# An attention-and-experts kernel on one core: TensorE in program order, output matmuls two tiles behind their energies

## The chip, the core and the metric

The kernel runs on one core of one Trainium2 chip. The core has a matrix engine (TensorE, PE in the profile, with its weight loads as PEld), three elementwise engines (VectorE or DVE, ScalarE or ACT, GpSimd or POOL), and a sync engine (SP), whose queue issues most of the transfers here. The engines run side by side and meet at semaphores. Matmuls write to PSUM, from which VectorE and ScalarE read. The metric is the device time of one execution in microseconds; of several runs the median counts.

## The reference, cut to what is computed

There are four images of 32 channels and 128 x 128 pixels. Layer 0 folds each 2 x 2 block of pixels into channels (128 channels, 64 x 64 = 4096 positions) and lets every position attend to all positions of its image. So an image has 4096 rows of length 128, and the energy is the 4096 x 4096 matrix of their cosines. Layer 1 works on the same data as 4096 tokens of 128 numbers per image.

```python
def _L0_conv_ref(x, gamma):                      # per image
    xs = x.reshape(B, C, h, R, w, R).transpose(0, 1, 3, 5, 2, 4).reshape(B, C * R * R, h, w)
    q = xs.reshape(B, C * R * R, hw)
    energy = jnp.einsum('bci,bcj->bij', q, q)
    d = jnp.sqrt(jnp.diagonal(energy, axis1=1, axis2=2))
    energy = energy / (d[:, :, None] * d[:, None, :])
    attn = jax.nn.softmax(energy, axis=-1)
    out = jnp.einsum('bcj,bij->bci', q, attn).reshape(B, C * R * R, h, w)
    out = gamma * out + xs
    ...
# layer 1
t = t + _L1_attn_ref(_ln_t(t), Wk, Wq, Wv)       # linear attention: a 128x128 matrix per image
t = t + _L1_ffn_ref(_ln_t(t), router_w, router_b, expert_w, expert_b)   # top 2 of 8 experts
```

The energy is symmetric, and so is its exponential. The kernel computes only one half of it, in tiles of 128 x 512, and gets the other half by transposing tiles.

## The kernel before: the parts that are touched

All is f32. The kernel is written with a scheduler: the program emits instructions in an order, and the scheduler decides in which order each engine gets them, by its own estimate of when each is ready. On the chip the order of every engine is then fixed, and semaphores make it wait.

An image's 4096 rows are 32 blocks of 128, or `NCH` = 8 chunks of 512. For chunk `i` ("a row") the kernel goes over the diagonal chunk and over the chunks `jc < i`. For each of four blocks `j` of such a chunk ("a tile") it makes an energy `pe`, its exponential `pr` on ScalarE, and the output matmul into `po`, which sums up over the whole row. The output matmul is held in `pend` and emitted after the next tile's energy.

```python
    ps_e = ctx.enter_context(tc.tile_pool(name="ps_e", bufs=2, space=PSUM))   # pe
    ps_o = ctx.enter_context(tc.tile_pool(name="ps_o", bufs=1, space=PSUM))   # po
    ps_g = ctx.enter_context(tc.tile_pool(name="ps_g", bufs=1, space=PSUM))   # pg
    ps_t = ctx.enter_context(tc.tile_pool(name="ps_t", bufs=2, space=PSUM))   # all transposes, and others
    ps_y = ctx.enter_context(tc.tile_pool(name="ps_y", bufs=2, space=PSUM))   # py, gram
    # ... cut ...
        for i in range(NCH):
            po = ps_o.tile([P, CH], F32, tag="po", name=f"po_{b}_{i}")
            # ... cut: order of chunks, pend, given, values, below ...
            for jc in order:
                # ... cut ...
                for j in range(NJ):
                    t = NJ * jc + j
                    c0 = 0 if jc < i else P * j
                    pe = ps_e.tile([P, CH], F32, tag="pe", name=f"pe_{b}_{i}_{t}")
                    nc.tensor.matmul(pe[:, c0:], qn[jc][:, ts(j, P)], qn[i][:, c0:], start=True, stop=True)
                    pr = ppool.tile([P, CH], F32, tag="pr", name=f"pr_{b}_{i}_{t}")
                    nc.scalar.activation(pr[:, c0:], pe[:, c0:], AF.Exp, accum_out=sums[:, t, i : i + 1])
                    flush()
                    if j == 1:
                        pend.extend(given)
                        given.clear()
                    pend.append(partial(values, pr[:, c0:], t, c0, CH))
                    if jc < i:
                        nc.vector.transpose(Fb[:, :, :, j, :], pr)
                    own.append(pr)
                    if jc == i and j in (1, 2):
                        pend.append(partial(below, own, (2, 1) if j == 1 else (3,)))
                    clock[0] += 2 * (CH - c0) // P
                    if late and late[0][0] <= clock[0]:
                        clock[0] += NJ
                        if next(late[0][1], "done") == "done":
                            late.pop(0)
                    yield
                if jc < i:
                    # ... cut: 16 transfers G <- F on SyncE ...
                    late.append((clock[0] + LAG, transposed_share(b, st, i, jc, G)))
            pend.extend(given)
            flush()
            o = opool.tile([P, CH], F32, tag="o", name=f"o_{b}_{i}")
            nc.vector.tensor_copy(o, po)
            st["o"].append(o)
```

In the diagonal chunk only the upper half of the tiles is computed. `below` makes the lower half: it transposes parts of `pr` on TensorE into `ptd`, ScalarE copies them to `gd`, and these go into output matmuls too (`given`).

For the chunks left of the diagonal, the transposed tiles are needed for another row's output. VectorE transposes `pr` in 32 x 32 squares into `F`, sixteen transfers put the squares in their places in `G`, and later (`LAG` in the kernel's own count of TensorE work) four matmuls `pg` are made of it, one after each tile; ScalarE sums up each part of `G` into `junk`, and VectorE adds `pg` to the other row's `o`.

Between tiles (at the `yield`) other streams take steps: the preparation of the next image (transposes `ptq`, `ptn`, and squares, norms and scaling `ss`, `rn`, `qs` on VectorE and GpSimd), and layer 1 of the image before. A stream gets a stretch of the image, in per cent of its work, and a count of steps.

```python
        else:
            streams.append((layer1(b - 1, states[b - 1], False), 7, 97, 161))
```

Layer 1 divides the output by the row sums (`pbd`, `df`), adds it to the tokens `T`, takes each token's mean and variance (`bs_a`, `dm_a`, the power on GpSimd for `rsa`, then `nba`), normalises on ScalarE, eight tokens' columns at once, and forms a Gram matrix `pgram`:

```python
        for kc in range(6):
            if kc < 4:
                yield from divide(kc)
            if 1 <= kc < 5:
                yield from row_stats(f"a{b}", kc - 1, rsa, nba)
                yield
                for k in range(8 * kc - 8, 8 * kc):
                    normalise(xn[:, k, :], k, rsa, nba)
                yield
            if 2 <= kc:
                gram_rows(kc - 2)
                yield
```

Then follow the attention product `pat`, a second normalisation into `xg`, its transposes `ptf`, routing, and the experts: for each of 32 token blocks two matmuls `py` of 128 x 512, with the bias from `pbe` and the gates transposed by `ptg`. The last image's layer 1 runs alone, after all attention is done.

Of the kernel before, what the change touches and what calls it, by code (L numbers as in the profile page):

```python
# [10 lines left out]
F32 = mybir.dt.float32  # L11
# [8 lines left out]
def kernel(  # L20
# [35 lines left out]
    nc = tc.nc  # L56
    P = 128
# [3 lines left out]
    CH = 512  # L61
    NCH = N // CH
    NJ = CH // P
# [11 lines left out]
    opool = ctx.enter_context(tc.tile_pool(name="opool", bufs=NCH + 2))  # L75
# [6 lines left out]
    ps_o = ctx.enter_context(tc.tile_pool(name="ps_o", bufs=1, space=PSUM))  # L82
# [4 lines left out]
    def psum_t(name):  # L87
        return ps_t.tile([P, CH], F32, tag="pt", name=name)
# [71 lines left out]
    def prep(b, kc, st):  # L160
# [35 lines left out]
        for s, qs in enumerate(scaled):  # L196
# [5 lines left out]
            st.setdefault("qn", {})[2 * kc + s] = qn  # L202
            yield

    late = []
    clock = [0]
    LAG = 56
# [19 lines left out]
    def attend(b, st):  # L227

        qT, qn = st.setdefault("qT", {}), st.setdefault("qn", {})
        st["sums"] = sums = stat.tile([P, NB, NCH + 1], F32, tag="sums", name=f"sums_{b}")  # L230
        nc.gpsimd.memset(sums[:, :, NCH:], 0.0)
        st["o"] = []

        for i in range(NCH):
            po = ps_o.tile([P, CH], F32, tag="po", name=f"po_{b}_{i}")
            ending = b == B - 1 and i == NCH - 1
            order = list(range(i)) + [i] if ending else [i] + list(range(i))
            pend, given = [], []
            count = [0]
            total = NJ * (i + 1) + NJ - 1  # L240

            def values(w, blk, lo, hi, i=i, po=po, count=count, total=total):
                count[0] += 1
                nc.tensor.matmul(  # L244
                    po[:, lo:hi], qT[blk // NJ][:, blk % NJ, :], w, start=(count[0] == 1), stop=(count[0] == total)
                )

            def below(tiles, blks, i=i, given=given):

                pt = psum_t(f"ptd_{b}_{i}_{blks[0]}")  # L250
                gd = ppool.tile([P, CH], F32, tag="pr", name=f"gd_{b}_{i}_{blks[0]}")
                at = 0
                for ib in blks:
                    for j in range(ib):
                        nc.tensor.transpose(pt[:, at + P * j : at + P * j + P], tiles[j][:, ts(ib, P)], ident)  # L255
                    w = gd[:, at : at + P * ib]
                    nc.scalar.activation(
                        w, pt[:, at : at + P * ib], AF.Copy, accum_out=sums[:, NJ * i + ib, NCH:]
                    )
                    given.append(partial(values, w, NJ * i + ib, 0, P * ib))  # L260
                    at += P * ib

            def flush(pend=pend):
                while pend:
                    pend.pop(0)()

            for jc in order:
                if jc < i:
                    F = fpool.tile([P, 4, NJ, NJ, S], F32, tag="F", name=f"F_{b}_{i}_{jc}")
                    Fb = F.rearrange("p q ib j c -> p ib q j c")  # L270
                own = []
# [4 lines that stand above are left out]
                    nc.tensor.matmul(pe[:, c0:], qn[jc][:, ts(j, P)], qn[i][:, c0:], start=True, stop=True)  # L276
                    pr = ppool.tile([P, CH], F32, tag="pr", name=f"pr_{b}_{i}_{t}")
                    nc.scalar.activation(pr[:, c0:], pe[:, c0:], AF.Exp, accum_out=sums[:, t, i : i + 1])  # L278
                    flush()
                    if j == 1:  # L280
                        pend.extend(given)
                        given.clear()
                    pend.append(partial(values, pr[:, c0:], t, c0, CH))
                    if jc < i:
                        nc.vector.transpose(Fb[:, :, :, j, :], pr)  # L285
                    own.append(pr)
                    if jc == i and j in (1, 2):
                        pend.append(partial(below, own, (2, 1) if j == 1 else (3,)))
                    clock[0] += 2 * (CH - c0) // P
                    if late and late[0][0] <= clock[0]:  # L290
                        clock[0] += NJ
# [4 lines that stand above are left out]
                    G = gpool.tile([P, 4, NJ, P], F32, tag="G", name=f"G_{b}_{i}_{jc}")  # L296
                    for a in range(4):
                        for q in range(4):
                            nc.sync.dma_start(  # L299
                                G[ts(q, S), a].rearrange("p ib f -> p (ib f)"),  # L300
                                F[ts(a, S), q].rearrange("p ib j c -> p (ib j c)"),
                            )
                    late.append((clock[0] + LAG, transposed_share(b, st, i, jc, G)))
                    st["due"] = st.get("due", 0) + 1
            pend.extend(given)
            flush()
            o = opool.tile([P, CH], F32, tag="o", name=f"o_{b}_{i}")
            nc.vector.tensor_copy(o, po)
            st["o"].append(o)

    def finish_late():
        while late:
            for _ in late.pop(0)[1]:
                pass


    def layer1(b, st, alone):
# [51 lines left out]
        def normalise(dst, k, rs, nb):  # L369
            nc.scalar.activation(dst, T[:, k, :], AF.Identity, scale=rs[:, k, :], bias=nb[:, k, :])  # L370
# [40 lines left out]
        def gram_rows(u):  # L411
            for k in range(8 * u, 8 * u + 8):
                nc.tensor.matmul(pgram[:, :D], xn[:, k, :], xn[:, k, :], start=(k == 0), stop=(k == KT - 1))  # L413
# [6 lines that stand above are left out]
                yield  # L420
                for k in range(8 * kc - 8, 8 * kc):
                    normalise(xn[:, k, :], k, rsa, nba)
                yield
            if 2 <= kc:
                gram_rows(kc - 2)
                yield
                if alone:
                    transpose_rows(2 * kc - 4)
                    transpose_rows(2 * kc - 3)
# [139 lines left out]
        for g in range(KT // 4):  # L569
# [5 lines left out]
            for jj in range(2):  # L575
                tmp = work.tile([P, 2, 4, D], F32, tag="wide", name=f"tmp_{b}_{g}_{jj}")
                for jk in range(2):
                    j = 2 * jj + jk
                    k = 4 * g + j
# [26 lines left out]
    states = [{} for _ in range(B)]  # L606
# [6 lines left out]
        pass  # L613
    carried = []

    for b in range(B):

        streams = list(carried)
        carried = []
        if b == 0:  # L620
            for kc, begin, end in ((1, 0, 5), (2, 6, 20), (3, 25, 45)):
                streams.append((prep(0, kc, states[0]), begin, end, 10))
            streams.append((setup_weights(), 50, 60, 4))
        else:
            streams.append((layer1(b - 1, states[b - 1], False), 7, 97, 161))
        if b + 1 < B:
            nxt = states[b + 1]
            streams.append((prep(b + 1, 0, nxt), 66, 84, 10))
            streams.append((prep(b + 1, 1, nxt), 85, 99, 10))
            carried.append((prep(b + 1, 2, nxt), 2, 20, 10))  # L630
            carried.append((prep(b + 1, 3, nxt), 30, 50, 10))
        done = [0] * len(streams)
        start = clock[0]
        for _ in attend(b, states[b]):
            t = 100 * (clock[0] - start) / UNITS
            for n, (steps, begin, end, count) in enumerate(streams):
                while t >= begin and done[n] * (end - begin) < (t - begin) * count:
                    next(steps, None)
                    done[n] += 1
        for steps, *_ in streams:  # L640
            for _ in steps:
                pass
    finish_late()
    last = states[B - 1]
    for _ in layer1(B - 1, last, True):
        pass
# [38 lines left out]
```

## Time and profile before

| | before |
|---|---|
| device time, median of 3 | 1890.58 us (1890.11 to 1890.69) |
| span of the profiled execution | 1886.6 us |
| mean granted TensorE clock | 0.983 |
| matmul records on TensorE | 5474 |
| ScalarE exp, 128x512 | 560 ns mean, and 199 ns to read its sum |
| VectorE transposes `F` | 704 ns mean, 448 of them |
| transfers `G` from `F` | 1792, 64 KB each |

The profile is one execution. In a timeline each line has the start, the time in us, the engine, the line of the kernel, the operation, what it writes and reads, its shape and how many records are merged; in brackets stand the idle time of that engine before it and what ended it. An f32 matmul of 128 x 512 appears as two records, a transpose as one. In the slices of the page each digit is a fortieth of the span, in tenths. Since TensorE is nearly always at work, the small gaps between its records matter more here than the shares.

### The profile page before, as it was taken

To read this page: it belongs to the slowest core of one execution; us is meant where nothing else is said; L and a number is where in the kernel's file an instruction comes from. 1 tells how busy PE (TensorE), PEld (TensorE's weight loads), DVE (VectorE), ACT (ScalarE), POOL (GpSimd) and SP (SyncE) were. 2 spreads that over 40 slices of the span, in tenths; PEclk is the share of its full clock that TensorE was granted. 3 is DMA by queue.
4 is the path that set the end of the run, shared out by engine and by line. 5 is a ranking of instruction groups with operands and counts; after the bars stand their busy time and mean duration, and the time that the engine had idled before them with its cause. 6 is when DMAs were issued, how large, how long until landed. Compare 5 with 4: busy or idle time off the path is not lost.

```text
span 1886.6 us, 21105 instructions
## 1 busy us (share of the span) xinstructions
PE 1799.0 (95%) x5474; PEld 915.4 (49%) x5474; DVE 909.5 (48%) x2201; ACT 974.6 (52%) x3117; POOL 293.7 (16%) x279
## 2 busy tenths in 40 slices
PE   6999999998999999999999999999899999999678
PEld 4444544454555444455555444445465544444533
DVE  3343224345364454636355455453536445554576
ACT  3454444446457454555556655454554755554455
POOL 0000000002010122212000022220300012221336
PEclk9999999999999999999999999999999999999789
DMA  5333343332233232342233323234233223335001
GB/s 119 80 84 87 78 104 91 89 89 64 61 95 83 65 89 65 86 105 64 64 85 81 92 62 90 68 88 99 53 79 81 72 63 92 81 74 119 1 11 34
DMA packets 142247, 145.68 MB, mean 77 GB/s; under 512 B 32528, under 2 KB 84784, under 8 KB 142128
## 3 DMA queue, kind: packets, MB, share of 16 engines
q1 hardware_dynamic: 138496, 142.73, 31.5%
q10 hardware_dynamic: 3632, 1.60, 0.4%
q8 instruction: 45, 0.74, 0.2%
q14 instruction: 74, 0.61, 0.1%
HBM read 18.38 MB, written 8.39 MB: 14 GB/s over the span
## 4 chain that ended last, share of the span: by engine, by line
PE 81%; DVE 7%; SPq 4%; POOL 3%; ACT 2%; DMA 1%; issue 1%; ACTq 0%; POOLq 0%; DVEq 0%
PE po L244 23%; PE pe L276 20%; PE pg L213 18%; PE py L588 5%; PE py L581 5%; SPq L299 4%; PE pbe L571 1%; PE pat L468 1%; PE pgram L413 1%; DVE F L285 1%; PE ptd L255 1%; POOL rsa L111 1%; DVE df L387 1%; POOL T L395 1%; PE ptn L199 1%
## 5 line engine op out<-in xcount | busy, mean ns | idle before, releaser
L278 ACT ACTIVATE pr<-pe 128x512 f32<-128x512 f32 (+1 forms) x576 | 322.7, 560 | 519.6 <-PE pe L276 513.9
L244 PE MATMUL po<-pr,qT 128*128 128x512 f32 (+3 forms) x1152 | 551.1, 561 | 16.4 <-ACT pr L278 11.6
L285 DVE STREAM_TRANSPOSE F<-pr 128x512 f32<-128x512 f32 x448 | 311.4, 704 | 354.0 <-ACT pr L278 336.5
L276 PE MATMUL pe<-qn,qn 128*128 128x512 f32 x896 | 459.7, 595 | 0.0
L213 PE MATMUL pg<-G,qT 128*128 128x512 f32 x896 | 440.8, 594 | 1.7 <-DVE o L223 1.6
L244 PEld LDWEIGHTS po<-pr,qT 128*128 128x128 f32 x1152 | 213.3, 191 | 249.0 <-issue 182.9
L218 ACT ACTIVATE junk<-G 128x512 bf16<-128x512 f32 x448 | 277.1, 626 | 3.6 <-DMA G<-F 2.8
L213 PEld LDWEIGHTS pg<-G,qT 128*128 128x128 f32 x896 | 167.4, 191 | 196.0 <-issue 186.8
L590 ACT ACTIVATE tmp<-py,gate 128x128 f32<-128x128 f32 x512 | 146.3, 368 | 172.1 <-PE py L588 171.1
L583 DVE SCALAR_TENSOR_TENSOR acc<-py,gate,acc 128x128 f32<-128x128 f32 x512 | 177.7, 349 | 118.3 <-PE py L581 104.6
L276 PEld LDWEIGHTS pe<-qn,qn 128*128 128x128 f32 x896 | 160.9, 191 | 145.3 <-issue 144.4
L223 DVE TENSOR_TENSOR o<-o,pg 128x512 f32<-128x512 f32 x112 | 76.6, 684 | 184.4 <-PE pg L213 183.7
L594 POOL TENSOR_TENSOR tmp<-tmp 128x512 f32<-128x512 f32 x64 | 81.2, 1269 | 534.6 <-ACT tmp L590 534.6
L581 PE MATMUL py<-ew_sb,xn 128*128 128x512 f32 x256 | 132.7, 601 | 1.9 <-ACT tmp L590 1.2
L588 PE MATMUL py<-ew_sb,xn 128*128 128x512 f32 x256 | 131.9, 597 | 2.2 <-DVE acc L583 1.4
L278 ACT ACTIVATION_READ_ACCUMULATOR pr<-pe 128x1 f32 x576 | 114.5, 199 | 0.0
L111 POOL TENSOR_TENSOR rn<-ss,neg_half 128x8 f32<-128x8 f32 x16 | 26.2, 1639 | 500.4 <-DVE ss L185 500.4
L276 PE MATMUL pe<-qn 128*128 128x512 f32 (+3 forms) x256 | 90.3, 444 | 0.0
L218 ACT ACTIVATION_READ_ACCUMULATOR junk<-G 128x1 f32 x448 | 88.5, 198 | 0.0
L370 ACT ACTIVATE xn<-T,nba,rsa 128x128 f32<-128x128 f32 x128 | 51.9, 481 | 55.1 <-DVE nba L367 55.1
L111 POOL TENSOR_TENSOR rsf<-dm_f,neg_half 128x8 f32<-128x8 f32 x16 | 26.3, 1642 | 342.5 <-DVE dm_f L365 342.5
L588 PEld LDWEIGHTS py<-ew_sb,xn 128*128 128x128 f32 x256 | 48.5, 191 | 61.9 <-issue 53.0
(121 smaller groups left out, 1416.5 us busy)
## 6 DMA issues: line engine op xcount, KB each, us to landing
G<-F SPq DMA_DIRECT2D x1792, 64.0 KB, 2.0
xx<-in_x_dram SPq DMA_DIRECT2D x64, 128.0 KB, 2.8
T<-in_x_dram SPq DMA_DIRECT2D x16, 512.0 KB, 7.1
out_dram<-acc SPq DMA_DIRECT2D x128, 64.0 KB, 1.8
ew_sb<-in_L_ffn_expert_w_dram ACTq DMA_DIRECT2D x1, 512.0 KB, 5.4
raw_w<-in_L_attn_Wv_dram ACTq DMA_DIRECT2D x1, 512.0 KB
raw_w<-in_L_attn_Wk_dram ACTq DMA_DIRECT2D x1, 256.0 KB
raw_w<-in_L_attn_Wq_dram ACTq DMA_DIRECT2D x1, 256.0 KB
```

The lines of the kernel that those rows point to most:

```text
L213: nc.tensor.matmul(pg.rearrange("p (a f) -> p a f", a=4), st["qT"][i][:, ib, :], G[:, :, ib], start=(ib == 0), stop=(ib == NJ - 1),)
L218: nc.scalar.activation(junk, G[:, :, ib], AF.Copy, accum_out=st["sums"][:, NJ * i + ib, jc : jc + 1])
L223: nc.vector.tensor_tensor(o, o, pg.rearrange("p (a j c) -> p a j c", a=4, c=S), ALU.add)
L244: nc.tensor.matmul(po[:, lo:hi], qT[blk // NJ][:, blk % NJ, :], w, start=(count[0] == 1), stop=(count[0] == total))
L276: nc.tensor.matmul(pe[:, c0:], qn[jc][:, ts(j, P)], qn[i][:, c0:], start=True, stop=True)
L278: nc.scalar.activation(pr[:, c0:], pe[:, c0:], AF.Exp, accum_out=sums[:, t, i : i + 1])
L285: nc.vector.transpose(Fb[:, :, :, j, :], pr)
L581: nc.tensor.matmul(py, xn[:, k, :], ew_sb[:, 0:4, :], start=True, stop=True)
L583: nc.vector.scalar_tensor_tensor(acc[:, j, :], py[:, ts(e, D)], gate[:, k, e : e + 1], acc[:, j, :], ALU.mult, ALU.add)
L588: nc.tensor.matmul(py, xn[:, k, :], ew_sb[:, 4:8, :], start=True, stop=True)
L590: nc.scalar.activation(tmp[:, jk, e, :], py[:, ts(e, D)], AF.Copy, scale=gate[:, k, 4 + e : 5 + e])
L594: nc.gpsimd.tensor_tensor(tmp[:, :, 0:2], tmp[:, :, 0:2], tmp[:, :, 2:4], ALU.add)
```

## The change

Two things are changed together. First, from the first image's attention on, TensorE is taken out of the scheduler's hands: it gets its instructions in the order in which the program emits them. Second, the program's own distance between an energy and its output matmul is made longer: a list `waiting`, shared by all rows and images, holds what follows from a tile, and it is emitted when two more tiles' energies stand ahead. At the end of a row nothing is flushed any more; the copy of `po` follows whichever output matmul turns out to be the row's last. The accumulator `po` is taken when the row's first output matmul is emitted. The values of the lower half of the diagonal block (`gd`) follow one tile after their transposes. With that go two small settings: normalisation gives way after every four instead of eight, and the steps of layer 1 are counted as 165 in place of 161.

The purpose is that TensorE never stands waiting for ScalarE's exp or for the turn of a row or an image.

```diff
@@ attend
+    waiting = []
     late = []
@@
-            po = ps_o.tile([P, CH], F32, tag="po", name=f"po_{b}_{i}")
             ending = b == B - 1 and i == NCH - 1
             order = list(range(i)) + [i] if ending else [i] + list(range(i))
-            pend, given = [], []
-            count = [0]
-            total = NJ * (i + 1) + NJ - 1
-
-            def values(w, blk, lo, hi, i=i, po=po, count=count, total=total):
-                count[0] += 1
+            row = {"left": NJ * (i + 1) + NJ - 1}
+
+            def values(w, blk, lo, hi, i=i, row=row):
+                if "po" not in row:
+                    row["po"] = ps_o.tile([P, CH], F32, tag="po", name=f"po_{b}_{i}")
+                    start = True
+                else:
+                    start = False
+                row["left"] -= 1
                 nc.tensor.matmul(
-                    po[:, lo:hi], qT[blk // NJ][:, blk % NJ, :], w, start=(count[0] == 1), stop=(count[0] == total)
+                    row["po"][:, lo:hi], qT[blk // NJ][:, blk % NJ, :], w, start=start, stop=(row["left"] == 0)
                 )
+                if row["left"] == 0:
+                    o = opool.tile([P, CH], F32, tag="o", name=f"o_{b}_{i}")
+                    nc.vector.tensor_copy(o, row["po"])
+                    st["o"].append(o)
@@ below
-                    given.append(partial(values, w, NJ * i + ib, 0, P * ib))
+                    waiting[-1].append(partial(values, w, NJ * i + ib, 0, P * ib))
@@ a tile
-                    flush()
-                    if j == 1:
-                        pend.extend(given)
-                        given.clear()
-                    pend.append(partial(values, pr[:, c0:], t, c0, CH))
+                    if len(waiting) == 2:
+                        for f in waiting.pop(0):
+                            f()
+                    waiting.append([partial(values, pr[:, c0:], t, c0, CH)])
                     ...
-                        pend.append(partial(below, own, (2, 1) if j == 1 else (3,)))
+                        waiting[-1].append(partial(below, own, (2, 1) if j == 1 else (3,)))
@@ end of a row
-            pend.extend(given)
-            flush()
-            o = opool.tile([P, CH], F32, tag="o", name=f"o_{b}_{i}")
-            nc.vector.tensor_copy(o, po)
-            st["o"].append(o)
@@ finish_late
+        while waiting:
+            for f in waiting.pop(0):
+                f()
@@ layer 1, normalisation
                 for k in range(8 * kc - 8, 8 * kc):
                     normalise(xn[:, k, :], k, rsa, nba)
-                yield
+                    if k % 4 == 3:
+                        yield
@@ ahead of the loop over images
+    ctx.enter_context(tc.manual_schedule(engines={mybir.EngineType.PE}))
@@ streams
-            streams.append((layer1(b - 1, states[b - 1], False), 7, 97, 161))
+            streams.append((layer1(b - 1, states[b - 1], False), 7, 97, 165))
```

## The prediction

> **What bounds the kernel now.** I read the page first: busy shares, then the slices, then the chain.
>
> ```profile
> PE 1799.0 (95%) x5474; PEld 915.4 (49%) x5474; DVE 909.5 (48%) x2201; ACT 974.6 (52%) x3117; POOL 293.7 (16%) x279
> ...
> PEclk9999999999999999999999999999999999999789
> ...
> PE 81%; DVE 7%; SPq 4%; POOL 3%; ACT 2%; DMA 1%; issue 1%; ACTq 0%; POOLq 0%; DVEq 0%
> ```
>
> TensorE is the bound: 95% busy, 81% of the chain, clock full until the tail. So nothing that another engine does can bring much, and the question is how much of TensorE's time is not work. The 95% does not tell: records overlap and their ends are modelled. Start to start is safer; in the timeline of TensorE's own records:
>
> ```profile
> 600.29 1.02 PE L244 MATMUL po<-pr,qT 128*128 128x512 f32 x2
> 601.15 1.02 PE L213 MATMUL pg<-G,qT 128*128 128x512 f32 x2
> 602.00 1.02 PE L276 MATMUL pe<-qn,qn 128*128 128x512 f32 x2
> ```
>
> Each 128x512 f32 matmul is two records and takes 0.857 us from start to start, 0.43 per pass, 0.84 ns a column. Taking 0.833 ns a column for a pass at full clock, I summed all 5474 records by their shapes: 1737 us. First start to last end is 9.6 to 1878.3 us, 1869 us. So about 131 us are not matmul time. By stretch (start to start, less the need of the shape): 9 us before 20 us, 73 us between 20 and 1733, 49 us in 1733 to 1823 (the last image's layer 1, alone), under 1 after. Of the 73, 31 lie in 20 to 455 (22 of them after 290, around the first change of image), 15 in 800 to 1000, 15 in 1250 to 1450; the long middles of images 1 to 3 lose 2 to 6 each. About 14 of the 73 are only the half per cent by which a real pass is longer than my 0.833. Single gaps over 0.15 us add up to 44 us, and only those can a new order touch. They divide so: output matmul waiting for its exp 16; transposes of the diagonal block (`ptd`) waiting for `gd` 10; matmuls at half clock just after such gaps 5; prep transposes (`ptn`) waiting for `qs` 4; output matmul waiting for the row's copy out of `po` 4; the rest 5.
>
> The worst ones, in the timelines of TensorE and of ScalarE:
>
> ```profile
> 896.50 0.39 PE L276 MATMUL pe<-qn 128*128 128x128 f32 x2
> 900.33 0.47 PE L255 MATMUL ptd<-ident,pr 128*128 128x128 f32 x1 [3.45 <-ACT gd L257]
> ```
>
> ```profile
> 896.38 2.80 ACT L370 ACTIVATE xn<-T,nba,rsa 128x128 f32<-128x128 f32 x7 [3.89 <-DVE nba L367]
> 899.08 0.36 ACT L278 ACTIVATE pr<-pe 128x256 f32<-128x256 f32 x1
> ```
>
> TensorE stands 3.45 us because ScalarE stood 3.89 us for `nba`, then ran seven normalisations (2.80 us), and only then the exp and `gd` that TensorE wanted. It recurs in image 3 at 1347 (5.3 us).
>
> **What the Trainium skill says.** "Perfetto Trace Analysis", section Per-instruction lifecycle, says that a matmul's end is an estimate from its size; the trace agrees (1.02 us listed for two passes, 0.857 between starts). The same section says that TensorE reorders only weight loads and that the other engines run strictly in order; the trace agrees: the ready exp of 899.08 stood behind the normalisations. So the order in the program decides, before as after. "TensorE: Matmul & The Clock Gate", Part 1, says the clock falls to half after an idle window of about 3.4 us; the trace agrees where it matters: after the 3.45 us gap the timeline shows 1.92 us for two records of 128x512 where 1.02 is normal. I found no statement on how far apart producer and consumer should stand.
>
> **The change part by part.** No matmul is added or removed: the sum by shapes is again 1737 us.
>
> *Distance of two tiles.* Before, the built order has, between the end of an energy matmul and the start of its output matmul, a median of 3.0 us of other TensorE work in images 1 to 3 (1.7 in image 0), under 2 us for 161 of 576 tiles. After, it is 5.8 us (5.1), and under 2 us for 2 of 576. The exp needs 0.56 + 0.20 us plus some 0.4 for the two hops, so 2 us is enough when ScalarE is free and 5 us also when it is late by one burst. I expect 13 of the 16 us back. The energy buffer does not become the limit: between an energy matmul and the second next, which takes its buffer, stand 4.7 us in the median (4.9 before).
>
> *Across rows and images.* The row's end no longer empties the pipe. But `po` has one buffer: the next row's first output matmul waits for the copy. In the trace the copy ends 1.32 us after the start of the last pass, 0.89 after its 0.43 us, and the next matmul can start 0.16 later: 1.05 us of other work is needed. Before, the order has 1.1 to 4.9 us there. After, 5 of 31 changes of row have 0.43, 3 have 0.85, most 1.28, the rest 2 to 3. Stall: 5 x 0.62 + 3 x 0.2 = 3.7 us, and about 2 where VectorE (48% busy) is in another operation. 6 in place of 4: 2 us lost.
>
> *Program order and smaller bursts.* `ptd` is spread over two tiles and its values stand one tile on (median 2.6 us, under 1 us once; before 7.4, but under 1 us ten times). Normalisations yield every four. Yet in the built order ScalarE still has up to eight between two exps, and 20 of them (0.40 us each) with five exps (0.76) and four `junk` (0.83) over five tiles, 15 us for perhaps 13 of TensorE: late by 2 or 3 us, within the new distance. Of the 10 us at `ptd` I expect 8 back, of the 5 at half clock 4, of the 4 at `ptn` 3.5 (prep is now in step with the program, not bunched at the image's end), of the rest 2.
>
> *Program order costs.* (a) Streams: a step of layer 1 comes every 2.3 us, and `ptf` follows its normalisation by one step, about what four of 0.40 and an exp need. 1.5 us an image in three images: 5. (b) `pg` waits for its 16 transfers. In the trace their issue starts 1.5 us after the energy matmul at the earliest and takes 10.0, and landing takes 2.0: 13.5 us. Before, image 0 has 17 to 36 us of other work there; after, 13.2 to 19.6. Mostly enough: 3 us lost. (c) Tail: before, six expert matmuls and one `pbe` (7 x 0.86 = 6 us) run while routing is under way, and 58 follow the last `ptf`. After, all 64 follow. Less is in ScalarE's way in exchange: 4 us lost.
>
> Sum: 13 + 8 + 4 + 3.5 + 2 = 30.5 gained; 2 + 5 + 3 + 4 = 14 lost; net 16 to 17. 1890.6 - 16.6 = 1874; I give 1872, as some of the small gaps must go too.
>
> **The rivals.** *The gaps go and nothing comes in their place*: 44 us and a few of the small ones, 1845. For it: distance doubles nearly everywhere. Against it: ScalarE's waits for `nba` come from GpSimd's 1.65 us power and the VectorE chain, untouched. *The transfer queue takes over in image 0*: one group of `pg` comes every 4 x (3 x 0.857) = 10.3 us and its issue takes 10.0 to 11, and other transfers share the queue. If each of the 28 groups waits 1 us: 25 us lost more, 1897. For it: the queue is the only thing nearly full there. Against it: every row has a diagonal block without `pg` in which the queue catches up. *In-order matmuls stall all along*: 0.3 us for each of some 250 steps of layer 1 in three images would be 75 us on the images, 1935. Against it: the two `py` buffers still have 3.8 us in the median between reuses.
>
> **Range and chances.** The touchable 44 us and a tail that may move by 5 either way limit the gain: over 2% means 38 us, nearly all of it without a new loss, 0.11. Slower by over 2% needs a stall at every step, 0.04. 0.85 for within 2%. Range 1852 to 1891: full gain less a little, to no gain.
>
> **What would show it.** Right: waits of `po` for `pr` fall from 11.6 (TensorE) and 38.5 us (weight load) to a quarter; no `ptd` gap over 2 us near 900 and 1350; waits of `po` for the copy rise from 3.3 us to some 6; chain share of PE up by one or two points. Wrong: `pg` waiting for G in image 0 by more than 5 us; `ptf`, `py` or `pbd` waiting for ScalarE or VectorE by more than 10 us in the images; the last `ptf` moving by more than 5 us against the end. The prediction fails as a whole if the middles of the images, which lose 2 to 6 us now, lose 15.

## The result: 1.0077 times the time before, and the profile after

| | before | after |
|---|---|---|
| device time, median | 1890.34 us (1887.04 to 1890.69, 4 runs) | 1904.3 us (1903.09 to 1905.04, 4 runs) |
| ratio, 95% interval | | 1.0077 (1.006 to 1.0095) |
| span of the profiled execution | 1886.6 us | 1901.3 us |
| first to last matmul on TensorE | 9.6 to 1878.3 us | 9.6 to 1893.0 us |

The change made the kernel slower by 0.8%. The prediction was 1872 us, 1852 to 1891, and the result lies outside of it. From the page of the changed kernel: the busy shares, and the chain by engine.

```profile
PE 1797.7 (95%) x5474; PEld 912.4 (48%) x5474; DVE 906.5 (48%) x2201; ACT 983.2 (52%) x3117; POOL 294.9 (16%) x279
...
PE 79%; DVE 8%; POOL 4%; issue 3%; ACT 3%; DMA 2%; SPq 1%; ACTq 0%; POOLq 0%; DVEq 0%
```

The busy time is the same within 1.3 us in a kernel 14.7 us longer. TensorE's share of the chain went from 81% to 79%: it works as much and stands more. For whom it stands is in the list of TensorE's waits (total us, times, the longest). First the kernel before, then after.

```profile
PE po L244 <- ACT pr L278: 11.6, 11, 1.9
...
PE ptd L255 <- ACT gd L257: 9.0, 3, 5.1
...
PE po L244 <- DVE o L308: 3.3, 2, 2.1
...
PE pg L213 <- DVE o L223: 1.6, 2, 0.8
```

```profile
PE ptd L262 <- ACT gd L264: 20.9, 32, 1.7
...
PE pg L214 <- DVE o L224: 16.3, 13, 2.8
...
PE po L247 <- DVE o L252: 7.2, 11, 1.1
```

(The lines left out are of the first 20 us or of the last layer 1, but for 3.0 us at one `ptn` of before and single waits under 1 us.) The waits for `pr`, which the change was made against, are gone from the list. Three others stand in their place, and the first occurs exactly 32 times: once in each diagonal block of each image.

To weigh the waits I use the same account as the prediction: start to start of the matmul records, less what the shape needs, put down to what released the later one. The four images, from the first energy to the first `pbd` of the last layer 1, gaps over 0.06 us, in us:

| TensorE's next matmul, and whom it waited for | before | after |
|---|---|---|
| output `po`, for exp | 16.1 | 0 |
| `ptd`, for the copy `gd` on ScalarE | 10.8 | 26.2 |
| `pg`, for VectorE's addition | 2.4 | 18.9 |
| output `po`, for VectorE's copy of the row | 3.7 | 9.0 |
| `ptn`, for `qs` | 3.1 | 0 |
| all losses of the four images, small ones too | 74.4 | 87.0 |
| loss in the last layer 1, alone | 48.2 | 50.4 |

The two last lines account for the difference: 12.6 + 2.2 = 14.8 us, against 14.7 in the ends of TensorE's work.

**The wait that occurs 32 times.** TensorE's timeline in row 4 of image 1 after the change, and ScalarE's:

```profile
496.63 0.81 PE L247 MATMUL po<-pr,qT 128*128 128x384 f32 x2
497.27 0.38 PE L262 MATMUL ptd<-ident,pr 128*128 128x128 f32 x2
498.22 0.33 PE L262 MATMUL ptd<-ident,pr 128*128 128x128 f32 x1 [0.56 <-ACT gd L264]
498.39 1.02 PE L214 MATMUL pg<-G,qT 128*128 128x512 f32 x2
```

```profile
497.69 0.38 ACT L264 ACTIVATE gd<-ptd 128x256 f32<-128x256 f32 x1 [0.23 <-PE ptd L262]
497.97 0.19 ACT L264 ACTIVATION_READ_ACCUMULATOR gd<-ptd 128x1 f32 x1
```

`below` writes two transposes into the PSUM tile `ptd`, has ScalarE copy them to `gd`, and then writes a third transpose into another part of the same tile. The program's dependencies are by tile: the third must wait for the copy. It needs 0.11 us and the two before it 0.21, and TensorE stands 0.73 us between them, or up to 1.8 where ScalarE is late. The scheduler had put other work between them in every diagonal block; 18 waits for the copy were left, 15 of them under 0.2 us. In the kernel before, in the last row of the last image:

```profile
1728.51 0.38 PE L255 MATMUL ptd<-ident,pr 128*128 128x128 f32 x2
1728.73 1.02 PE L213 MATMUL pg<-G,qT 128*128 128x512 f32 x2
1729.59 0.27 PE L255 MATMUL ptd<-ident,pr 128*128 128x128 f32 x1
```

Program order says what the program says: the third transpose directly behind the copy.

**The wait for `pg`.** VectorE in image 1 after the change, ahead of the addition that frees the one `pg` buffer, and TensorE, which waits for it:

```profile
433.28 0.17 DVE L367 SCALAR_TENSOR_TENSOR nba<-sv_a,rsa 128x8 f32<-128x8 f32 x1 [1.75 <-POOL rsa L111]
433.37 0.70 DVE L287 STREAM_TRANSPOSE F<-pr 128x512 f32<-128x512 f32 x1
434.08 2.79 DVE L387 TENSOR_TENSOR df<-o,pbd 64x512 f32<-64x512 f32 x4
436.90 0.71 DVE L287 STREAM_TRANSPOSE F<-pr 128x512 f32<-128x512 f32 x1
437.65 0.69 DVE L224 TENSOR_TENSOR o<-o,pg 128x512 f32<-128x512 f32 x1
```

```profile
434.85 1.02 PE L247 MATMUL po<-pr,qT 128*128 128x512 f32 x2
438.39 1.12 PE L214 MATMUL pg<-G,qT 128*128 128x512 f32 x2 [2.52 <-DVE o L224]
```

The last pass of the `pg` group before started at 433.56 and is listed as ended at 434.15, so the addition could have run at about 434.2. It ran at 437.65. Ahead of it in VectorE's order stood four divisions and a transpose, and before these VectorE had stood 1.75 us for GpSimd. The same stand comes at 894 and 1350 us. Another of 2.1 us comes at 543, 1000 and 1456 us; at 543 VectorE has other work ahead of the addition, from 538.84 to 542.16: the scaling `qs` for the next image and the short operations of the routing.

### The profile page after: what moved, and what is told of

Same layout as the page of the kernel before. It is cut to its first block, busy times and chain, and to the rows that moved or that the text cites. A ratio compares the mean times of both kernels' runs of the same rounds, so it can differ in the third digit from the quotient of the medians.

```text
span 1901.3 us, 21103 instructions
## 1 busy us (share of the span) xinstructions
PE 1797.7 (95%) x5474; PEld 912.4 (48%) x5474; DVE 906.5 (48%) x2201; ACT 983.2 (52%) x3117; POOL 294.9 (16%) x279
## 4 chain that ended last, share of the span: by engine, by line
PE 79%; DVE 8%; POOL 4%; issue 3%; ACT 3%; DMA 2%; SPq 1%; ACTq 0%; POOLq 0%; DVEq 0%
PE po L247 21%; PE pe L279 20%; PE pg L214 17%; PE py L582 6%; PE py L589 6%; PE pbe L572 2%; PE pgram L413 1%; SPq L301 1%; PE ptd L262 1%; PE pat L469 1%; DVE F L287 1%; POOL rsf L111 1%; DMA G<-F 1%; DVE df L387 1%; POOL T L395 1%
## 5 line engine op out<-in xcount | busy, mean ns | idle before, releaser
L214 PE MATMUL pg<-G,qT 128*128 128x512 f32 x896 | 460.8, 597 | 16.7 <-DVE o L224 16.3
L111 POOL TENSOR_TENSOR rn<-ss,neg_half 128x8 f32<-128x8 f32 x16 | 26.2, 1640 | 443.0 <-DVE ss L185 443.0
```

The costliest lines, as they stand in the source:

```text
L214: nc.tensor.matmul(pg.rearrange("p (a f) -> p a f", a=4), st["qT"][i][:, ib, :], G[:, :, ib], start=(ib == 0), stop=(ib == NJ - 1),)
```

## The experiments

All times are medians on the chip, with the ratio to the kernel before measured beside them. Losses are by the account above.

### The shared tile

`a1_ptd` changes `below` alone:

```diff
                 for ib in blks:
                     for j in range(ib):
                         nc.tensor.transpose(pt[:, at + P * j : at + P * j + P], tiles[j][:, ts(ib, P)], ident)
+                    at += P * ib
+                at = 0
+                for ib in blks:
                     w = gd[:, at : at + P * ib]
                     nc.scalar.activation(w, pt[:, at : at + P * ib], AF.Copy, accum_out=sums[:, NJ * i + ib, NCH:])
```

> The changed kernel, only `below` emits its three transposes first and then the two copies. Theory 1 (shared tile): the 0.73 to 1.8 us gap before the third `ptd` transpose of each diagonal block, 32 times, 26 us in all, is there because program order puts it directly behind a copy of the same PSUM tile; without it 1904.3 - 24 = 1880 us, range 1875 to 1886, and no gap at `ptd` over 0.3 us. Rival (VectorE): the gaps only move to the values of `gd` behind it, TensorE stands for ScalarE there; then under 8 us, 1896 or more.

Measured: 1882.37 us, ratio 0.9965 (0.9953 to 0.9978), 21.9 us less than the changed kernel. No wait of `ptd` for the copy is left. The same place in TensorE's timeline, one line in place of two:

```profile
489.71 0.81 PE L247 MATMUL po<-pr,qT 128*128 128x384 f32 x2
490.36 0.49 PE L262 MATMUL ptd<-ident,pr 128*128 128x128 f32 x3
490.69 1.02 PE L214 MATMUL pg<-G,qT 128*128 128x512 f32 x2
```

Theory 1 holds. The other two waits did not move: 18.9 us at `pg`, 9.6 at `po`.

The same edit on the kernel before, `a4_before_ptd`:

> The kernel before, only `below` emits its three transposes first and then the two copies; the scheduler orders TensorE. Theory 1: the 10.8 us at `ptd` in the kernel before is partly the same wait, partly ScalarE late by normalisations; 2 to 8 us faster, 1882 to 1889 us. Rival: the scheduler had already put other work there, nothing changes, 1889 to 1893.

Measured: 1881.73 us, 0.9965 (0.9952 to 0.9978), 7.8 us less by the medians (the kernel before ran at 1889.5 beside it) and 6.6 by the ratio, the most that theory 1 allowed. The gap at `ptd` fell from 10.8 to under 0.5 us, though the waits for exp rose from 16.1 to 23.7: part of what `ptd` had stood for, late normalisations on ScalarE, TensorE now stands for at an output matmul.

### Order and distance apart

`a2_lag_only` leaves out the one line of program order; `a3_order_only` adds only that line to the kernel before.

```diff
-    ctx.enter_context(tc.manual_schedule(engines={mybir.EngineType.PE}))      # a2_lag_only, from after
+    ctx.enter_context(tc.manual_schedule(engines={mybir.EngineType.PE}))      # a3_order_only, to before
```

> The changed kernel without program order: the two-tile distance and the smaller bursts stay, the scheduler orders TensorE again. Theory 1 (the order costs, the distance gains): the scheduler fills the `ptd` gap and the waits for exp are few; below the kernel before, 1870 to 1886 us. Rival (distance itself costs, by `po` turning late or by `pr` buffers held longer): 1893 or more.

> The kernel before with TensorE in program order, one tile of distance, flush at the end of a row. Theory 1: `ptd` gaps 26 us as in the changed kernel, and exp waits come on top: after each energy only 0.9 to 2.6 us stand before its output matmul, and every row ends in a stand of 1 to 2 us, so 1935 to 1980 us. Rival (distance is worth little): 1900 to 1912, as the changed kernel.

Measured: `a2_lag_only` 1886.88 us, 0.9987 (0.9978 to 0.9995); `a3_order_only` 1919.34 us, 1.0163 (1.0148 to 1.0178). The first is just outside what was expected: the distance gains little where the scheduler orders. The second lies between the two ranges. It is slower than the changed kernel, but by 15 us and not by 31 or more: waits for exp are 20.4 us in all, less than the 1 to 2 us that I had put at the end of every one of 32 rows. `ptd` takes 31.0 us in it.

The two with the shared tile repaired, `c3_lag_ptd` and `e1_order_ptd`:

> Distance of two tiles and small bursts without program order (a2_lag_only, 1886.9 us), with the shared-tile fix. If distance and scheduler work together, its 7 us at `ptd` go: 1880 us, range 1877 to 1883, as a1_ptd and a4_before_ptd. If the order alone is what made the wait, nothing: 1885 to 1888.

> Program order with one tile of distance (a3_order_only, 1919.3 us), with the shared-tile fix. If the shared tile costs the same at any distance, 31 us go: 1888 us, range 1883 to 1893, and 20 us of waits for exp stay. If exp waits take its place: 1897 or more.

Measured: `c3_lag_ptd` 1880.27 us, 0.995 (0.9936 to 0.9965), as expected. `e1_order_ptd` 1874.01 us, 0.9922 (0.9907 to 0.9937): 45 us less than without the repair and 9 below the range. The repair took off 29.8 us at `ptd`, 5.5 at exps, and 11 in the rest of the images: 4 at `pg`, the others in small gaps and matmuls at half clock.

| | one tile | two tiles and smaller bursts |
|---|---|---|
| scheduler's order | 1890.3 (before) | 1886.9 |
| program order | 1919.3 | 1904.3 (after) |
| scheduler's order, tile repaired | 1881.7 | 1880.3 |
| program order, tile repaired | 1874.0 | 1882.4 |

The kernel before itself ran at medians of 1887.6 to 1890.3 us beside the different versions, so differences of 2 or 3 us in this table are rough. The table overturns my first reading, "the order costs, the distance gains". That holds only with the shared tile. Repaired, program order gains 7.7 us at one tile, and the longer distance in program order costs 8.4.

Was it the distance, or the bursts? `f1_order_burst` is `e1_order_ptd` with normalisation giving way every four and 165 steps:

```diff
                 for k in range(8 * kc - 8, 8 * kc):
                     normalise(xn[:, k, :], k, rsa, nba)
-                yield
+                    if k % 4 == 3:
+                        yield
...
-            streams.append((layer1(b - 1, states[b - 1], False), 7, 97, 161))
+            streams.append((layer1(b - 1, states[b - 1], False), 7, 97, 165))
```

> e1_order_ptd (program order, one tile, shared-tile fix: 1874.0 us) with the smaller bursts of normalisation and 165 steps; it then differs from a1_ptd (1882.4 us) by the distance and the open end of rows alone. Theory 7 (the longer distance costs, as rows turn on the one `po` with too little between): 1871 to 1877 us. Rival (the smaller bursts cost): 1880 to 1885.

Measured: 1876.74 us, 0.994 (0.9925 to 0.9955), so theory 7. By the medians the bursts cost 2.7 us, which is within the two intervals, and the distance with the open row ends 5.6. At one tile TensorE's output matmuls stand 13.1 us for exp, 7.2 at `pg` and 5.1 at `po`; at two tiles 0, 18.9 and 9.6. So with the distance the waits for exp go, and 16.2 us come at `pg` and `po`.

### The turn of `po`

`b1_turn` is `a1_ptd` with the row's first output matmul held back one tile more:

```diff
-                    if len(waiting) == 2:
+                    held = 3 if jc == order[0] == i and j == 2 else 2
+                    while len(waiting) >= held:
                         for f in waiting.pop(0):
                             f()
```

> The shared-tile fix of the run a1_ptd (1882.4 us), and at a row's start the first output matmul is held back one tile more: between a row's last output matmul and the next row's first stand 0.64 to 4.6 us of other work in place of 0.43 to 3.1. Theory 2 (turn of `po`: one buffer, the copy needs 1.05 us): the 9.6 us that output matmuls stand for the copy fall to about 2; 1875 us, range 1872 to 1879. Rival (VectorE is simply late, wherever the turn stands): the wait moves to `pg` or stays, 1880 to 1885.

Measured: 1876.93 us, 0.9937 (0.9922 to 0.9951), 5.4 less than `a1_ptd`. Waits for the copy fell from 9.6 to 4.1. Theory 2 holds with a somewhat smaller size, but part of the wait moved: energies that wait for the exp of their buffer went from 1.1 to 4.8 us, and the images' losses in the traces fell by only 2.0.

### The tail

`b3_tail` is `a1_ptd` with program order for the loop over images only:

```diff
-    ctx.enter_context(tc.manual_schedule(engines={mybir.EngineType.PE}))
-    for b in range(B):
-        ...
-    finish_late()
+    with tc.manual_schedule(engines={mybir.EngineType.PE}):
+        for b in range(B):
+            ...
+        finish_late()
```

> The shared-tile fix of a1_ptd, program order only for the four images; the last image's layer 1 alone is ordered by the scheduler as before. Theory 4 (program order costs in the tail, as it holds expert matmuls back): TensorE's loss in the tail falls from 53 to 48 us; 1877 to 1880 us. Rival: the tail hangs on VectorE and GpSimd and the order is of no account, 1881 to 1884.

Measured: 1877.43 us, 0.9941 (0.9924 to 0.9957), 4.9 less; TensorE's loss in the tail fell from 53.1 to 47.0. The last `ptf` starts 76.5 us after the first `pbd` here and 77.4 in `a1_ptd`, but 58 expert matmuls follow it here and 64 there. So theory 4: the six held back, 6 x 0.86 = 5.1 us. The size is rough: with one and the same order the tail lost 50.4 us in the changed kernel, 53.1 in `a1_ptd` and 51.9 in `b1_turn`, and on top of the turn (`d1_turn_tail`, below) the same edit gained 3.1 us.

### Who makes VectorE late

`b2_pool` tests whether VectorE's stand for GpSimd's power delays the addition of `pg`. The bias moves behind the power, on GpSimd:

```diff
+            hm = stat.tile([P, 8, 1], F32, tag="hm", name=f"hm_{nm}_{u}")
+            nc.vector.tensor_scalar(hm, sv[:, :, 0:1], -0.5, None, ALU.mult)
             pow_neg_half(rs[:, :, 0], dm[:, :, 0])
-            nc.vector.scalar_tensor_tensor(nb, sv[:, :, 0:1], -0.5, rs, ALU.mult, ALU.mult)
+            nc.gpsimd.tensor_tensor(nb[:, :, 0], hm[:, :, 0], rs[:, :, 0], ALU.mult)
```

> The shared-tile fix of a1_ptd, and the bias `nba`, `nbf` of both normalisations is multiplied on GpSimd behind its power, so that VectorE does not stand 1.4 to 1.8 us for each power. Theory 3 (`pg` waits because VectorE stands for GpSimd ahead of the addition of `pg`): the 18.9 us of `pg` waiting for VectorE fall to 8 to 12; 1874 us, range 1870 to 1878. Rival (the addition is late because four divisions of 0.69 us stand ahead of it in VectorE's order): `pg` still waits 16 us or more, 1879 to 1884.

Measured: 1881.94 us, 0.9963 (0.9948 to 0.9978), and 21.1 us at `pg`, as the rival had it. Theory 3 falls. With turn and tail added, `b4_all`:

> All four together: shared-tile fix, longer turn, bias on GpSimd, tail by the scheduler. If the causes add up, 1882.4 - 7 - 8 - 4 = 1863 us, range 1857 to 1869. If they are one cause (VectorE late), they overlap: 1870 to 1876.

Measured: 1877.24 us, 0.9938 (0.9924 to 0.9953), slower than both ranges. VectorE's timeline in it, at the same place in image 1, shows why:

```profile
425.40 0.71 DVE L291 STREAM_TRANSPOSE F<-pr 128x512 f32<-128x512 f32 x1 [2.19 <-ACT pr L284]
426.15 2.79 DVE L393 TENSOR_TENSOR df<-o,pbd 64x512 f32<-64x512 f32 x4
428.97 0.71 DVE L291 STREAM_TRANSPOSE F<-pr 128x512 f32<-128x512 f32 x1
429.71 0.69 DVE L224 TENSOR_TENSOR o<-o,pg 128x512 f32<-128x512 f32 x1
```

VectorE no longer stands for GpSimd but 2.19 us for an exp, and the four divisions still stand ahead of the addition.

`c2_norm` (on `a1_ptd`) gives way after every two normalisations (`k % 2 == 1`, 173 steps). By that the scheduler put the addition ahead of the divisions.

> The shared-tile fix of a1_ptd, and normalisation gives way after every two instead of four (steps of layer 1 173 in place of 165); in VectorE's order the addition of `pg` then stands ahead of the four divisions. Theory 6 (ScalarE's normalisations make exps late, and `F` and the divisions then stand ahead of the addition): `pg` waits fall from 18.9 to 10 us or less; 1874 us, range 1870 to 1878. Rival: the waits move elsewhere, 1880 to 1885.

Measured: 1891.82 us, 1.0014 (1.0007 to 1.0021), 9.4 us slower than `a1_ptd` and outside both ranges. The waits at `pg` did fall, from 18.9 to 5.8; those at `po` rose from 9.6 to 27.5. TensorE and VectorE in image 1 of this run:

```profile
433.69 0.59 PE L282 MATMUL pe<-qn 128*128 128x256 f32 x2
440.72 2.07 PE L247 MATMUL po<-pr,qT 128*128 128x512 f32 x2 [6.43 <-DVE o L252]
```

```profile
435.47 1.65 DVE L359 BATCH_NORM_STATS2 bs_a<-T 128x6 f32<-128x128 f32 x8 [2.46 <-POOL T L398]
...
439.78 0.17 DVE L370 SCALAR_TENSOR_TENSOR nba<-sv_a,rsa 128x8 f32<-128x8 f32 x1 [1.76 <-POOL rsa L111]
439.97 0.69 DVE L252 COPY o<-po 128x512 f32<-128x512 f32 x1
```

The copy of `po` now stands behind the whole chain of one token group: addition to `T` on GpSimd, statistics, power, bias. With one buffer each for `po` and `pg`, VectorE's chain is felt at whichever stands behind it.

`c1_gap` (on `a1_ptd`) gives the addition more time in place of speeding it up:

```diff
                         if next(late[0][1], "done") == "done":
                             late.pop(0)
+                            if late and i <= 5:
+                                late[0] = (max(late[0][0], clock[0] + 16), late[0][1])
```

> The shared-tile fix of a1_ptd, and in rows 0 to 5 of each image a new group of `pg` starts one tile later after the last one has ended, so 1.7 us and more of other TensorE work lie between, for the addition that frees the one `pg` buffer. Theory 5 (distance: the addition has only an energy and an output matmul of time): `pg` waits fall from 18.9 us to 6; 1872 us, range 1868 to 1876. Rival (VectorE is behind by more than a tile, and the groups pile up): 1879 or more.

Measured: 1877.26 us, 0.9934 (0.992 to 0.9949). `pg` fell by 15.0 to 3.9 us as theory 5 had it, but `po` rose by 6.0 to 15.6 and waits of energies for exp by 6.7 to 7.8. The images' losses fell by 5.5 us: some two thirds of the gain moved on, and the time lies between the two ranges. In both runs the wait left one buffer and came back at the others.

### Together

`d1_turn_tail` is tile, turn and tail; `e2_gap_all` adds the gap; `e3_gap_pool` adds the bias on GpSimd.

> Shared-tile fix, longer turn of `po`, tail by the scheduler; the bias stays on VectorE. If b4_all was held back by the bias on GpSimd alone: 1876.9 - 5 = 1872 us, range 1869 to 1875. If turn and tail overlap: 1876 or more.

> d1_turn_tail (1873.8 us) with a tile between groups of `pg` in rows 0 to 5. If turn and gap each take their own wait, `pg` waits fall from 20.6 to 6 us and `po` waits stay at 4 to 6: 1865 us, range 1861 to 1869. If there is one cause behind both (VectorE late in rows 2 and 3), the wait moves to `po` or to exp: 1871 to 1876.

> e2_gap_all with the bias of the normalisations on GpSimd. With turn and gap in place, what is left of VectorE's delay is its stand for GpSimd's power ahead of the copy of `po`: another 3 us less than e2_gap_all. Rival, as in b2_pool: within 1.5 us of e2_gap_all, or slower.

Measured: 1873.84 us, 0.9915 (0.9898 to 0.9931); 1863.57 us, 0.9868 (0.9854 to 0.9883); 1860.59 us, 0.9853 (0.9837 to 0.987). Turn and gap together do what neither did alone: `pg` 4.5 us and `po` 7.6 in `e2_gap_all`. Waits of energies for exp are 9.3 there, now the largest. Only then is GpSimd's bias worth its 3.0 us; in `b4_all` it cost 3.4 against `d1_turn_tail`. These are TensorE's largest waits in `e3_gap_pool` inside the images, from the same list as above:

```profile
PE pe L282 <- ACT pr L284: 6.6, 6, 1.5
...
PE po L247 <- DVE o L252: 5.1, 5, 2.0
PE pg L214 <- DVE o L224: 4.0, 7, 0.8
```

Last, all repairs with one tile of distance, `f2_one_tile_all` (without the turn, for a row ends closed there):

> The same with a tile between groups of `pg` in rows 0 to 5, the bias on GpSimd and the tail by the scheduler: one tile of distance against two in e3_gap_pool (1860.6 us), which also has the longer turn. If distance is worth something once turn and gap are repaired: 1864 to 1872, with waits for exp of 8 us or more. If it is worth nothing: 1858 to 1863.

Measured: 1866.99 us, 0.9889 (0.9873 to 0.9906), with 14.5 us of waits for exp. So once `ptd`, `po` and `pg` are repaired, the longer distance (with its turn) is worth 6.4 us by the medians. `e3_gap_pool` is the fastest version measured, 1.5% faster than the kernel before.

## Why the prediction was wrong, step by step

**What bounds the kernel, and the most that can come**: right. TensorE was busy for 1799.0 us before and 1797.7 after, and no version gained more than 30 us, where single gaps add up to 44.

**Distance of two tiles, 13 of 16 us back**: right in kind, all 16.1 came back. As a saving it was small, since other waits took the place. Of the 16.1 us, 11.4 stood in seven waits at 433 to 439, 531, 884, 984, 1337 and 1436 us; `a1_ptd` stands 14.6 us for `pg` at 432, 535, 882, 985, 1333 and 1436. That these are the same delays, met one buffer on, is likely but not shown. With the tile repaired the distance cost 5.6 us before turn and gap were mended and gained 6.4 after. (The 560 ns of the table of before mix the diagonal's shorter exps; one of 128x512 takes 596 ns, which changes nothing here. The energy buffer was no limit in the changed kernel, as forecast, but is the largest wait in `e2_gap_all`.)

**"Of the 10 us at `ptd` I expect 8 back"**: the step that failed. 10.8 us became 26.2, 23 us away from 2.8. The part that I had in view came out: the two long gaps near 900 and 1350 us fell from 3.6 and 5.3 us to 1.8 each (at 907 and 1363), and none over 2 us is left. What I had not in view was a wait of 0.7 us or more in all 32 diagonal blocks. I looked at the distance between a `ptd` and the output matmul of its `gd`, and took the scheduler's spreading for granted. The order of the changed kernel had the third transpose directly behind the second, with a wait for ScalarE between: two copies from one tile that are interleaved with its writes are a chain of four steps across two engines. `a1_ptd` shows it: 22 us. With the 1904.3 - 21.9 = 1882.4 us it leaves, the result would have lain in the range.

**Turn of `po`, 6 in place of 4**: right in kind, mis-sized; 9.0, at 11 changes of row where 8 were forecast.

**What the sum left out: `pg` and its addition.** I asked of `pg` only whether its transfers had landed, and looked no further at its buffer. It has one, and program order puts the next group one energy and one output matmul after the last; 18.9 us in place of 2.4. Order alone does not make it: 7.0 us with program order alone (`a3_order_only`), 9.2 with the distance alone (`a2_lag_only`), 18.9 with both. `c1_gap` shows that one more tile takes away 15.0 of it, of which 5.1 are left in the time, and `c2_norm` that it is exchanged for waits at `po`.

**Half clock, 4 of 5 us back**: wrong by that measure, 5.4 us became 6.3; with small losses counted too it was 9.5 and 6.3. The stretches at half clock in the images now follow gaps at `pg`, near 439, 893, 1351 and 1457 us; before they followed gaps of four kinds. **Prep, 3.5 back**: right, 3.1 to 0. **Streams, 5 us lost**: wrong; no `ptf`, `py` or `pbe` waits in the images. **`pg` waiting for transfers in image 0, 3 lost**: wrong, 0.1 us. **Tail, 4 lost**: right; 2.2 in the loss account, and 4.9 by `b3_tail`.

So in place of gains of 30.5 stand 16.1 + 3.1 and 5.4 in all that is small, and in place of losses of 14 stand 15.4 at `ptd`, 16.5 at `pg`, 5.3 at `po` and 2.2 in the tail: 14.8 us lost.

Of the rivals, none was right. "In-order matmuls stall all along" was the nearest in kind: they stall in the images, but at three places and not at every step.

The Trainium skill's sentence that the engines run strictly in order ("Perfetto Trace Analysis", Per-instruction lifecycle) was used for ScalarE only. VectorE's five lines at 433 us show the same: the addition was ready at about 434.2 and ran at 437.65, after the divisions and the transpose that stood ahead of it.

Left open: why ScalarE and VectorE are late where TensorE still waits for them, some 22 us in the images of `e3_gap_pool`. A second buffer for `po` or `pg` was not tried either; the PSUM pools of the kernel have 2 + 1 + 1 + 2 + 2 tiles.

## What to carry to other kernels

Before an engine is taken out of a scheduler's hands, read the program's own order for every place where it goes to another engine and comes back to the same tile: write everything into the tile first, then let it be read. That edit was worth 6.6 and 7.8 us under the scheduler, 22 and 45 us without it.

When a wait is removed, look at the single buffers next to it: each needs as much other work between its last and its next use as its reader takes when it is late, not when it is free. Where a wait moves from one buffer to another under edits, as from `pg` to `po` and to exp here, measure the whole loss and not the one wait: look at what the engines that free these buffers have ahead of it.

## What the runs showed of the hardware that I had not expected

**The clock falls after less than an idle window.** The prediction took from the Trainium skill, "TensorE: Matmul & The Clock Gate", Part 1, that about 3.4 us of idling are needed. In the changed kernel the clock is at half for 3.41 us from 439.55 us, after a gap of 2.7 us. I took all the runs' stretches of 3.41 us that the clock keeps to, at full clock, and summed TensorE's idle time in each by the account above: of the 147 that were followed by a half-clock stretch the least idle has 2.06 us, of the 9838 that were not the most idle has 2.23, and only 13 of these exceed 2.06. So the measured limit is near 2.1 us of idle time in 3.41, in one gap or several. By an estimate from these stretches, one of 3.41 us at half clock costs up to 1.7 us more. Where page and runs differ, the runs decide.

**GpSimd's multiplication is not slow.** The power of 128x8 takes 1.65 us; the multiplication of the same size behind it, in `b4_all`, takes 0.20 us, against 0.17 for the bias on VectorE.

**A read of the sum is part of the wait.** After the copy to `gd` at 497.69 ScalarE's line of the accumulator ends at 498.16, and TensorE goes on at 498.22: 0.05 us after the read of the sum, 0.15 after the copy itself. All 32 waits at `ptd` end 0.05 us after the read, and the waits for VectorE at `po` and `pg`, where no sum is read, 0.05 us after its operation. The read starts before the copy's listed end, so it adds 0.09 us to the wait and not its whole 0.19.
